# A ceiling on the density planner's rate, and a rebuilt tail, in an attention-then-density kernel

## The chip, the cores and the metric

The kernel runs on one core of a Trainium2 chip. A core has five engines that work side by side, each through its own queue in order: TensorE (PE, matrix products), VectorE (DVE, elementwise work and reductions), ScalarE (ACT, functions such as exp and tanh), GpSimd (POOL) and SyncE (SP, which here issues the DMAs). They wait for each other by semaphores. The metric is the time of one execution on the device, in microseconds (us).

## The reference, cut to what matters

The input is x, 8 images of 192 channels by 64 x 64 pixels, fp32. Two layers follow each other, each with a group norm of 32 groups of 6 channels in front and a residual around it.

```python
# layer 0: attention over the 4096 pixels of an image, on the group-normed x
q, k, v = prelu(conv1x1(gn(x), w1, b1)), prelu(conv1x1(gn(x), w2, b2)), prelu(conv1x1(gn(x), wa, ba))
x = x + softmax(q^T k) v                      # q, k: 24 channels; v: 192
# layer 1: a small network per channel, evaluated at gn(x) - 0.5 and gn(x) + 0.5
def logits(y):                                # widths 1, 3, 3, 3, 1
    for i in range(4):
        y = softplus(m[i]) @ y + b[i]
        if i < 3:
            y = y + tanh(f[i]) * tanh(y)
    return y
lower, upper = logits(gn(x) - 0.5), logits(gn(x) + 0.5)
sign = -sign(lower + upper)
x = x + max(abs(sigmoid(sign * upper) - sigmoid(sign * lower)), 1e-6)
```

The norm in front of layer 1 needs the whole attention output of an image. So the density work (layer 1) of an image can only start when its attention has ended.

## The kernel before

**The stream.** After a short head the kernel runs 1024 steps (t = 0 to 1023; `last` is 1024): 8 images (`IMG` = 128 steps), each in 8 blocks of 512 queries with 16 steps (`STEPS`), a step being one part of the keys. Image numbers start at 0 here. In a step PE computes a score tile for the next step (L780, tile sc), a score tile 22 steps ahead for the row maximum (L708, tile mx) and the product of the exponentials with the values (L795, tile b). ACT takes the exponential (L784, e from sc). DVE reduces mx to a row maximum (L716). The mx tile has one buffer, so the next L708 waits for L716.

**The planner.** All other work is laid between the steps in Python, while the program is built. `at(t, fn, ...)` puts a function under step t in `due`. `work_off(t, rate)` runs what is due, starts a job in a free PSUM tile if it can, and then calls `density_step`. There each of DVE, ACT and PE has a credit that grows by a rate in each step; due work is charged to it, and so is each density operation. Because each engine's queue is in order, the order in which the planner emits instructions is the order in which they run.

**Density work.** `Unit(b, c, g, s)` is one half-image column c, one of three channel groups g, and one sign s (lower or upper): 12 units per image, worked off in the order of a deque, up to three at a time. A unit's operations go over tiles of 128 x 1024. In the usual form it takes 16 ACT operations (first-layer tanh L1005, linear part L1014, tanh L1020, scaled copies L1030) and 23 DVE operations (all at L1037: nine mixes, then gates and adds). In the form with `on_pe` the second layer's linear part and the nine mixes are three sums on PE (`product`, L978), each of four matrix products (x and three tanhs) with diagonal weights, in one of four two-bank PSUM tiles (`banks`); then come a tanh from PSUM (L986), a gate that reads PSUM and frees it (L996), and 11 more DVE operations. Before the change, all units of the last image but the first have this form. The diagonals are built on ACT (L876: nine per group from constants; L882: three per group from the last norm).

In the stream, the density work of image b is spread over image b+1: the rate is what is left divided by the steps until 15 steps into image b+2. Buffers for tiles are 17 (`bufs`); a unit may take one only if more are free than what older units still need (`need`).

**Endings.** When both units of a column and group are done, `ending` forms the likelihood. In the stream the sum, difference and product are on POOL; near the end `alone` does them on DVE (L1187, L1196, L1197), with tanh (L1192) and Abs (L1205) on ACT, and the last add into x (L1209), after which SP stores two halves of the partitions by DMA (L1213).

**The last norm.** After the last step, `finish` scales the attention output (L815, L819), transposes it on PE (L828), adds it into x (L837) and takes statistics (L442); `norm_end` then goes in steps: aggregate (L451), mean over the group on PE (L456), differences (L462 to L466), variance on PE (L471), its sum (L477, L478), a square root on ACT (L484), and the reciprocal with one correction step (L490 to L494), and at last the weights wn (L503) and bn (L506) of the density layers. Each step stands at least one planner step after the one before; a planner step after `last` works with `RATE` = 4.15 us of DVE credit.

Of the kernel before, what the change touches and what calls it, by code (L numbers as in the profile page):

```python
# [10 lines left out]
AF = mybir.ActivationFunctionType  # L11
ALU = mybir.AluOpType
# [5 lines left out]
def kernel(  # L18
# [43 lines left out]
    nc = tc.nc  # L62

    B, C, H, W = x.shape
    N = H * W
# [812 lines left out]
    def linear_diagonals(b):  # L878
        wn, bn = norms[b, 1]
        for g in range(3):  # L880
            for i in range(3):
                nc.scalar.activation(  # L882
                    diag[g][:, 9 + i, :], ident, AF.Copy, scale=wn[:, g, 1, i : i + 1]
                )

        for s in range(2):
            d, q = lower2[:, s], lower2[:, 2 + s]
            nc.vector.tensor_copy(d, cb[:, :, 6:9])
            for j in range(3):
                nc.vector.tensor_tensor(  # L890
                    q, wsp[:, :, 12 + j : 21 : 3],
                    bn[:, s, :, 1, j : j + 1].to_broadcast([128, 3, 3]), ALU.mult,
                )
                nc.vector.tensor_tensor(d, d, q, ALU.add)
        for t in (
            *turns, ps_sc.tile([128, 2, F], F32, tag="sc", name="sc_tail"),
            ps_mx.tile([128, 2, F], F32, tag="mx", name="mx_tail"),
        ):
            banks.append(t)
    zs = {}  # L900

    class Unit:
# [3 lines left out]
        def __init__(self, b, c, g, s):  # L906
            self.key = b, c, g, s
            self.at = {}
            self.buf = {}
            self.todo = {"DVE": deque(), "ACT": deque(), "PE": deque()}  # L910
            self.left = {"l": 6, "t": 9, "u": 0, "z": 1}
            self.held = {"l": 0, "t": 0, "u": 0, "z": 0}
            self.on_pe = b == B - 1 and c + g + s > 0
            add = self.add
            if self.on_pe:

                self.left.update(t=3, u=3)
                for i in range(3):
                    add("ACT", ("u", 0, i), [], self.tanh0, makes="u")
                for i in range(3):  # L920
                    add(
                        "PE", ("sum", i), [("u", 0, j) for j in range(3)], self.product,
                        frees=[("u", 0, j) for j in range(3)] if i == 2 else [],
                    )
                    add("ACT", ("l", 1, i), [("sum", i)], self.tanh1, makes="l")
                for i in range(3):
                    add("DVE", ("gate", 1, i), [("l", 1, i)], self.gate1)
            else:
                for i in range(3):
                    add("ACT", ("t", 0, i), [], self.tanh0, makes="t")  # L930
                    add("ACT", ("l", 1, i), [], self.linear, makes="l")
                for i in range(3):
                    for j in range(3):
                        add(
                            "DVE", ("mix", i, j), [("t", 0, j), ("l", 1, i)], self.mix,
                            frees=[("t", 0, j)] if i == 2 else [],
                        )
                    add("ACT", ("t", 1, i), [("mix", i, 2)], self.tanh, makes="t")
                for i in range(3):
                    add("DVE", ("gate", 1, i), [("t", 1, i)], self.gate, frees=[("t", 1, i)])  # L940
            for i in range(3):
# [193 lines left out]
    def ending(b, c, g):  # L1135
# [6 lines left out]
        def later(n, fn, *cost):  # L1142
            at(now[0] + n, fn, *cost)
# [38 lines left out]
        def alone():  # L1182

            s = cell["s"]

            def first():
                nc.vector.tensor_tensor(s, z[0], z[1], ALU.add)  # L1187
                later(1, second, 0.0, 2.1)

            def second():  # L1190
                for i in range(2):
                    nc.scalar.activation(z[i], z[i], AF.Tanh, scale=0.5)  # L1192
                later(1, third, 2.5)

            def third():
                nc.vector.tensor_tensor(z[0], z[1], z[0], ALU.subtract)  # L1196
                nc.vector.scalar_tensor_tensor(z[0], s, 0.0, z[0], ALU.not_equal, ALU.mult)  # L1197
                bufs.extend((s, z[1]))
                later(1, size, 0.0, 1.1)
                later(2, store, 1.3)  # L1200

            later(1, first, 1.25)

        def size():
            nc.scalar.activation(z[0], z[0], AF.Abs, scale=0.5)  # L1205

        def store():
            x_ = xc[b, c][:, g, :]
            nc.vector.scalar_tensor_tensor(x_, z[0], 1e-6, x_, ALU.max, ALU.add)  # L1209
            bufs.append(z[0])  # L1210
            for i in range(2):
                k = i * N // 2 + c * 2 * F
                nc.sync.dma_start(  # L1213
                    out=ov[b, :, g, k : k + 2 * F], in_=x_[R * i : R * i + R]
                )
            if g == 2:
                xc.pop((b, c))
                free["xc"] += 1
# [155 lines left out]
    for g in range(3):  # L1374
# [5 lines left out]

# [36 lines left out]
```

## Time and profile before

| what | us |
|---|---|
| median of three runs | 4846.51 |
| lowest and highest | 4843.33, 4850.05 |
| the profiled execution | 4845.56 |
| its span, first to last instruction | 4843.8 |
| PE busy | 4656.6 (96%) |
| DVE busy | 4260.6 (88%) |
| ACT busy | 3116.6 (64%) |
| POOL busy | 523.3 (11%) |

The profile is one execution, recorded instruction by instruction. The span is cut into 40 equal slices of about 121 us; in the rows of slices a digit is the busy share of an engine in tenths, and PEclk is the clock that PE was granted. A fp32 matrix product shows as two records. The chain of waits follows the work that ended last back from the end. In timelines a line has the start, the duration, the engine, the source line, the operation and tiles, and in brackets the idle time before it with the releaser.

The largest groups of the profile:

| line, engine | count | busy us | mean ns |
|---|---|---|---|
| L795 PE | 16384 | 2966.5 | 335 |
| L780 PE | 4096 | 1155.8 | 640 |
| L708 PE | 4008 | 1132.7 | 641 |
| L716 DVE | 1002 | 1222.4 | 1220 |
| L1037 DVE, three forms | 2076 | 2652.0 | 1277 to 1300 |
| L784 ACT | 1024 | 1044.9 | 1020 |

Back to back, operations overlap a little: four of L1037 took 4.88 us on the chain of waits, 1.22 each.

### The profile page before, as it was taken

What the parts mean: (1) busy time and instruction counts of PE and PEld (TensorE: products, weight loads), DVE (VectorE), ACT (ScalarE), POOL (GpSimd) and SP (SyncE); (2) the same over time, 40 slices, a digit from 0 to 9 for tenths busy, and PEclk for the clock granted to TensorE, in tenths of its full rate; (3) what the DMA queues carried; (4) which work ended last, traced back from release to release, by engine and by line L of the source; (5) the groups of instructions that cost most, each with busy time, mean ns of one, the idle gap of its engine ahead of it and who ended that gap; (6) DMA issues with size and microseconds to landing.
All of it is one profiled execution on the core that took longest, in us unless ns stands there. A gap on an engine that the chain in (4) does not pass through costs nothing.

```text
span 4843.8 us, 68352 instructions
## 1 busy us (share of the span) xinstructions
PE 4656.6 (96%) x28384; PEld 3443.8 (71%) x28384; DVE 4260.6 (88%) x4378; ACT 3116.6 (64%) x3581; POOL 523.3 (11%) x506
## 2 busy tenths in 40 slices
PE   7999999999999999999999999999999999999496
PEld 5777777777777777777777777777777777777132
DVE  5433369999999999999999999999999999998887
ACT  2332247676767667777667766776777767777665
POOL 0000001111112111111111101111111111211000
PEclk9999999999999999999999999999999999999698
DMA  2101010001100111111110111110111100000000
GB/s 61 38 23 24 18 48 25 25 24 40 42 20 24 40 35 34 31 32 29 38 29 26 37 39 29 31 37 15 35 42 28 27 24 22 10 23 5 9 13 13
DMA packets 109163, 138.55 MB, mean 29 GB/s; under 512 B 17074, under 2 KB 82100, under 8 KB 108852
## 3 DMA queue, kind: packets, MB, share of 16 engines
q1 hardware_dynamic: 107616, 133.81, 11.0%
q8 instruction: 222, 3.64, 0.3%
q14 instruction: 89, 0.73, 0.1%
q10 hardware_dynamic: 1236, 0.37, 0.0%
HBM read 100.58 MB, written 29.36 MB: 27 GB/s over the span
## 4 chain that ended last, share of the span: by engine, by line
PE 79%; DVE 14%; ACT 4%; issue 1%; POOL 1%; DMA 0%; ACTq 0%; DVEq 0%; POOLq 0%
PE b L795 48%; PE sc L780 18%; DVE d L1037 9%; PE b L669 4%; DVE rm L716 3%; PE b L978 2%; PE b L620 1%; PE sc_tail L978 1%; PE mx_tail L978 1%; PE b L828 1%; ACT e L784 1%; PE mx L708 1%; ACT d L1005 1%; ACT d L1030 1%; ACT d L1020 1%
## 5 line engine op out<-in xcount | busy, mean ns | idle before, releaser
L795 PEld LDWEIGHTS b<-v,e 128*128 128x128 f32 x16384 | 2662.2, 191 | 779.1 <-issue 775.3
L795 PE MATMUL b<-v,e 128*128 128x193 f32 x16384 | 2966.5, 335 | 0.0
L784 ACT ACTIVATE e<-sc 128x1024 f32<-128x1024 f32 x1024 | 1044.9, 1020 | 1444.1 <-PE mx L708 1409.3
L716 DVE TENSOR_REDUCE rm<-mx 128x1 f32<-128x1024 f32 x1002 | 1222.4, 1220 | 445.9 <-PE mx L708 440.8
L780 PE MATMUL sc<-q,k 25*128 25x512 f32 x4096 | 1155.8, 640 | 22.4 <-ACT e L784 22.3
L708 PE MATMUL mx<-k,q 24*128 24x512 f32 x4008 | 1132.7, 641 | 14.1 <-DVE rm L716 13.8
L1037 DVE SCALAR_TENSOR_TENSOR d<-d,wsp,d 128x1024 f32<-128x1024 f32 x768 | 984.6, 1283 | 45.7 <-ACT d L1030 34.4
L1037 DVE SCALAR_TENSOR_TENSOR d<-d,lc,d 128x1024 f32<-128x1024 f32 x765 | 986.5, 1300 | 16.5 <-ACT d L1014 5.1
L1037 DVE SCALAR_TENSOR_TENSOR d<-d,tf,d 128x1024 f32<-128x1024 f32 x543 | 680.9, 1277 | 2.5 <-ACT d L1020 2.5
L1020 ACT ACTIVATE d<-d 128x1024 f32<-128x1024 f32 x543 | 568.0, 1053 | 65.3 <-DVE d L1037 64.7
L780 PEld LDWEIGHTS sc<-q,k 25*128 25x128 f32 x4096 | 306.4, 183 | 249.9 <-issue 189.1
L1125 POOL MEMSET pause<- 128x1 f32 x240 | 23.5, 98 | 3888.0 <-DVE d L1037 3888.0
L1030 ACT ACTIVATE d<-d,cb,wsp 128x1024 f32<-128x1024 f32 x351 | 433.4, 1235 | 2.3 <-DVE d L1037 1.7
L1005 ACT ACTIVATE d<-xc,bn,wn 128x1024 f32<-128x1024 f32 x288 | 353.6, 1234 | 12.2 <-DVE bn L506 11.4
L708 PEld LDWEIGHTS mx<-k,q 24*128 24x128 f32 x4008 | 299.9, 183 | 30.3 <-DVE rm L716 29.1
L1014 ACT ACTIVATE d<-xc,bn,wn 128x1024 f32<-128x1024 f32 x255 | 314.7, 1234 | 0.0
L1160 POOL TENSOR_TENSOR d<-d,d 128x512 f32<-128x512 f32 x80 | 173.1, 2164 | 0.7 <-issue 0.2
L1172 POOL TENSOR_TENSOR d<-d,d 128x512 f32<-128x512 f32 x80 | 167.3, 2092 | 0.4 <-issue 0.4
L1180 POOL TENSOR_TENSOR d<-d,d 128x512 f32<-128x512 f32 x80 | 161.7, 2021 | 1.9 <-ACT d L1030 0.3
L669 PE MATMUL b<-wv,xi 64*128 64x192 f32 x1344 | 139.5, 340 | 0.2 <-ACT pra L596 0.2
L669 PEld LDWEIGHTS b<-wv,xi 64*128 64x128 f32 x1344 | 106.5, 186 | 25.7 <-issue 20.2
L978 PE MATMUL b<-d,v 128*128 128x512 f32 x204 | 95.9, 622 | 17.1 <-ACT d L1005 17.1
(154 smaller groups left out, 2064.4 us busy)
## 6 DMA issues: line engine op xcount, KB each, us to landing
xi<-in_x_dram SPq DMA_DIRECT2D x280, 192.0 KB, 3.4
xc<-in_x_dram SPq DMA_DIRECT2D x64, 384.0 KB, 7.0
out_dram<-xc SPq DMA_DIRECT2D x96, 256.0 KB, 3.1
q<-qd SPq DMA_DIRECT2D x128, 128.0 KB, 2.6
k<-kq SPq DMA_DIRECT2D x64, 64.0 KB, 1.9
qd<-kq SPq DMA_DIRECT2D x64, 64.0 KB, 2.1
d<-in_x_dram SPq DMA_DIRECT2D x16, 192.0 KB, 4.6
d<-in_wat_dram ACTq DMA_DIRECT2D x2, 144.0 KB
```

Of the source, the lines that this page charges most:

```text
L669: nc.tensor.matmul(pv[:, s, 0:C], lhsT=t[p, g, k * 128 : k * 128 + 128] if g < 3 else one_row[p], rhs=wf["v", b][p, g, :] if g < 3 else wf ...
L708: nc.tensor.matmul(sc[:, s, :], lhsT=tile_of(qt[b, n // 2], n, j)[r], rhs=kt[b][r, u : u + F], start=True, stop=True,)
L716: nc.vector.tensor_reduce(out=rowmax[b, n][:, j, k : k + 1], in_=sc, axis=AX.XY, op=ALU.max)
L780: nc.tensor.matmul(sc[:, s, :], lhsT=kt[b][r, k : k + 128], rhs=qt[b, n // 2][r, :, u : u + 256], start=True, stop=True,)
L784: return lambda: nc.scalar.activation(e, sc, AF.Exp)
L795: nc.tensor.matmul(a[:, j, 0 : C + 1], lhsT=e[:, s, j * 128 : j * 128 + 128], rhs=v[:, s, p % 4, :], start=p == 0 and s == 0 and j % 2 == ...
L978: nc.tensor.matmul(out[:, h, :], lhsT=diag[g][:, 3 * i + n - 1 if n else 9 + i, :], rhs=src[:, h * F : h * F + F], start=n == 0, stop=n == 3,)
L1005: nc.scalar.activation(self.buf[k], self.src(), AF.Tanh, bias=bn[:, s, g, 0, i : i + 1], scale=wn[:, g, 0, i : i + 1],)
L1014: nc.scalar.activation(self.buf[k], self.src(), AF.Identity, bias=bn[:, s, g, 1, i : i + 1], scale=wn[:, g, 1, i : i + 1],)
L1020: nc.scalar.activation(self.buf[k], self.buf["l", k[1], k[2]], AF.Tanh)
L1030: nc.scalar.activation(self.buf[k], self.buf["l", n - 1, 0], AF.Identity, bias=offset, scale=wsp[:, g, w : w + 1],)
L1037: nc.vector.scalar_tensor_tensor(dst, src, factor, dst, ALU.mult, ALU.add)
```

## The change

It has three parts.

1. In the stream, the rate of `density_step` is at most `MOST` = 3.3.
2. `need` counts a unit's last-layer buffer (kind z) only once the unit has made its last layer-2 add.
3. The tail is rebuilt. All 12 units of the last image take the PE form. The nine constant diagonals per group are made one per step inside the last image's stream (the third group's end two steps before `last`), no longer after it; those from the norm are made for group 0 first, the others three and six steps later, and the small offsets of `lower2` move into `tail`, one step later. After `last`, planner steps have 1.3 instead of 4.15 until the last norm is ready. Up to four units are in flight instead of three, always oldest first. The very last ending works in two halves of 512 columns, with four smaller stores instead of two.

```diff
+    MOST = 3.3
...
-    def diagonals(g):
-
-        d = vtiles.pop(0).rearrange("p a b c -> p (a b c)")[:, 0 : 12 * 128]
-        d = d.rearrange("p (k n) -> p k n", k=12)
-        diag.append(d)
+    def diagonals(g, t):
+
+        def one(k):
+            if k == 0:
+                d = vtiles.pop(0).rearrange("p a b c -> p (a b c)")[:, 0 : 12 * 128]
+                diag.append(d.rearrange("p (k n) -> p k n", k=12))
+            nc.scalar.activation(diag[g][:, k, :], ident, AF.Copy, scale=lc[:, g, k : k + 1])
+
         for k in range(9):
-            nc.scalar.activation(d[:, k, :], ident, AF.Copy, scale=lc[:, g, k : k + 1])
+            at(t + k, lambda k=k: one(k), 0.0, 0.4)
...
-            self.on_pe = b == B - 1 and c + g + s > 0
+            self.on_pe = b == B - 1
...
             most = dict(self.left, t=max(0, min(self.left["t"], 1 - self.held["t"])))
+            if ("add", 2, 2, 2) not in self.at:
+
+                most.update(z=0, p=0)
             return sum(most.values())
...
             rate = left * COST["DVE"] / max(1, (units[0].key[0] + 2) * IMG + 15 - t) + OTHER
+            rate = min(rate, MOST)
...
-            order = list(range(min(3, len(units))))
-            if len(units) == 2:
+            order = list(range(min(3 if t < last else 4, len(units))))
+            if len(units) == 2 and t < last:
...
         if b == B - 1:
-            linear_diagonals(b)
+            linear_diagonals(b, 0)
+            for g in (1, 2):
+                at(now[0] + 3 * g, lambda g=g: linear_diagonals(b, g), 0.0, 1.2)
+            at(now[0] + 1, lambda: tail(b), 2.2)
...
             s = cell["s"]
+            parts = halves if (b, c, g) == (B - 1, 1, 2) else [slice(0, 2 * F)]
 
             def first():
-                nc.vector.tensor_tensor(s, z[0], z[1], ALU.add)
+                for n in parts:
+                    nc.vector.tensor_tensor(s[:, n], z[0][:, n], z[1][:, n], ALU.add)
...
-            for i in range(2):
-                k = i * N // 2 + c * 2 * F
-                nc.sync.dma_start(
-                    out=ov[b, :, g, k : k + 2 * F], in_=x_[R * i : R * i + R]
-                )
+                for i in range(2):
+                    k = i * N // 2 + c * 2 * F
+                    nc.sync.dma_start(
+                        out=ov[b, :, g, k + n.start : k + n.stop], in_=x_[R * i : R * i + R]
+                    )
...
+            else:
+
+                diagonals(0, t + 93)
+                diagonals(1, t + 104)
+                diagonals(2, last - 11)
...
-    for g in range(3):
-        at(t + 4 + g, lambda g=g: diagonals(g))
     while due or units or jobs or loads:
-        work_off(t, RATE)
+
+        work_off(t, RATE if (B - 1, 1) in norms else 1.3)
         t += 1
```

More of the change, by code (lines that the diff above doesn't have):

```diff
@@ L868, with linear_diagonals, tail @@
     lower2 = mm.rearrange("p g n -> p (g n)")[:, 0:36].rearrange("p (s g i) -> p s g i", s=4, g=3)
-    def diagonals(g):
-        d = vtiles.pop(0).rearrange("p a b c -> p (a b c)")[:, 0 : 12 * 128]
-        d = d.rearrange("p (k n) -> p k n", k=12)
-        diag.append(d)
+    def diagonals(g, t):
[4 more added lines that the diff above has]
+            nc.scalar.activation(diag[g][:, k, :], ident, AF.Copy, scale=lc[:, g, k : k + 1])
         for k in range(9):
-            nc.scalar.activation(d[:, k, :], ident, AF.Copy, scale=lc[:, g, k : k + 1])
-    def linear_diagonals(b):
+            at(t + k, lambda k=k: one(k), 0.0, 0.4)
+    def linear_diagonals(b, g):
         wn, bn = norms[b, 1]
-        for g in range(3):
-            for i in range(3):
-                nc.scalar.activation(
-                    diag[g][:, 9 + i, :], ident, AF.Copy, scale=wn[:, g, 1, i : i + 1]
-                )
+        for i in range(3):
+            nc.scalar.activation(
+                diag[g][:, 9 + i, :], ident, AF.Copy, scale=wn[:, g, 1, i : i + 1]
+            )
+    def tail(b):
+        wn, bn = norms[b, 1]
         for s in range(2):
@@ L1184, in alone @@
             s = cell["s"]
+            parts = halves if (b, c, g) == (B - 1, 1, 2) else [slice(0, 2 * F)]
             def first():
-                nc.vector.tensor_tensor(s, z[0], z[1], ALU.add)
+                for n in parts:
+                    nc.vector.tensor_tensor(s[:, n], z[0][:, n], z[1][:, n], ALU.add)
                 later(1, second, 0.0, 2.1)
             def second():
-                for i in range(2):
-                    nc.scalar.activation(z[i], z[i], AF.Tanh, scale=0.5)
+                for n in parts:
+                    for i in range(2):
+                        nc.scalar.activation(z[i][:, n], z[i][:, n], AF.Tanh, scale=0.5)
@@ L1193, in second @@
                 later(1, third, 2.5)
             def third():
-                nc.vector.tensor_tensor(z[0], z[1], z[0], ALU.subtract)
-                nc.vector.scalar_tensor_tensor(z[0], s, 0.0, z[0], ALU.not_equal, ALU.mult)
+                for n in parts:
+                    y = z[0][:, n]
+                    nc.vector.tensor_tensor(y, z[1][:, n], y, ALU.subtract)
+                    nc.vector.scalar_tensor_tensor(y, s[:, n], 0.0, y, ALU.not_equal, ALU.mult)
                 bufs.extend((s, z[1]))
-                later(1, size, 0.0, 1.1)
@@ L1200, in third, with size @@
-                later(2, store, 1.3)
+                later(1, lambda: size(parts), 0.0, 1.1)
+                later(2, lambda: store(parts), 1.3)
             later(1, first, 1.25)
[L1204 to L1209, printed above, removed]
-            bufs.append(z[0])
-            for i in range(2):
-                k = i * N // 2 + c * 2 * F
-                nc.sync.dma_start(
-                    out=ov[b, :, g, k : k + 2 * F], in_=x_[R * i : R * i + R]
-                )
+        def size(parts=(slice(0, 2 * F),)):
+            for n in parts:
+                nc.scalar.activation(z[0][:, n], z[0][:, n], AF.Abs, scale=0.5)
@@ L1216, in store @@
+        def store(parts=(slice(0, 2 * F),)):
+            for n in parts:
+                x_ = xc[b, c][:, g, n]
+                nc.vector.scalar_tensor_tensor(x_, z[0][:, n], 1e-6, x_, ALU.max, ALU.add)
+                for i in range(2):
+                    k = i * N // 2 + c * 2 * F
+                    nc.sync.dma_start(
+                        out=ov[b, :, g, k + n.start : k + n.stop], in_=x_[R * i : R * i + R]
+                    )
+            bufs.append(z[0])
             if g == 2:
@@ L1373 @@
     homes[:] = [(turns[1], [0, 0])]
-    for g in range(3):
-        at(t + 4 + g, lambda g=g: diagonals(g))
     while due or units or jobs or loads:
-        work_off(t, RATE)
+        work_off(t, RATE if (B - 1, 1) in norms else 1.3)
         t += 1
```

## The prediction

> **What bounds the kernel now.** I read the slices of the page first, then the windows of the last 364 us, then the order of time on each engine at two places: an image boundary and the tail.
>
> ```profile
> PE   7999999999999999999999999999999999999496
> DVE  5433369999999999999999999999999999998887
> PEclk9999999999999999999999999999999999999698
> ```
>
> From slice 7 to 37 both PE and DVE show nines, so either could be the bound. The starts of the exp activations tell them apart: most of the 1024 steps are 3.88 us apart, which is PE's pace (L795 2.81 on the chain, L780 and L708 side by side, 1.06). DVE idles about 16 us per image there. But at a boundary of two images the chain leaves PE and runs over DVE (1778 to 1813 us). The timelines of DVE and of PE (start, us, engine and line, count, and in brackets the wait before):
>
> ```profile
> 1805.04 0.55 DVE L442 BATCH_NORM_STATS2 st<-xi 128x6 f32<-128x384 f32 x1
> 1805.50 3.66 DVE L1037 SCALAR_TENSOR_TENSOR d<-d,tf,d 128x1024 f32<-128x1024 f32 x3
> 1809.08 2.67 DVE L1037 SCALAR_TENSOR_TENSOR d<-d,lc,d 128x1024 f32<-128x1024 f32 x2
> 1811.66 1.22 DVE L716 TENSOR_REDUCE rm<-mx 128x1 f32<-128x1024 f32 x1
> ```
>
> ```profile
> 1812.94 1.69 PE L708 MATMUL mx<-k,q 24*128 24x512 f32 x4 [2.77 <-DVE rm L716]
> 1814.56 5.52 PE L795 MATMUL b<-v,e 128*128 128x193 f32 x16
> ```
>
> Five density operations stand between two reduces, so L708 waits 2.77 us for a free bank; the next L795 then takes 5.52 instead of 2.88. By the exp starts the six steps 12 to 17 of image 3 take 34.7 us; at PE's pace they would take 23.3. The same shape stands at the starts of images 2 to 6, five times. At image 7, where the burst is weaker, they take 28.3.
>
> The end, in four stages (columns: span, then busy us and count of PE, PEld, DVE, ACT, POOL, clock, DMA):
>
> ```profile
> 4480.00:4531.20 51.20, 2.71 (x10) 2.14 (x10) 49.32 (x57) 32.75 (x55) 0.00 (x0) 0.53 0.04 10
> 4531.20:4564.40 33.20, 24.80 (x49) 10.43 (x50) 27.96 (x38) 25.61 (x30) 0.00 (x0) 0.76 0.06 17
> 4564.40:4807.20 242.80, 213.71 (x481) 92.06 (x479) 199.90 (x163) 158.41 (x147) 0.00 (x0) 0.96 0.03 9
> 4807.20:4843.80 36.60, 0.07 (x1) 0.00 (x0) 26.02 (x22) 14.05 (x13) 0.00 (x0) 0.54 0.11 29
> ```
>
> For 51 us after the last attend (4479.6, call it E) PE stands still and DVE is full: the steps of the last norm lie in one DVE queue with image 6's density.
>
> ```profile
> 4479.61 0.18 DVE L815 RECIPROCAL rc<-b 128x4 f32<-128x4 f32 x1
> ...
> 4520.02 0.15 DVE L477 TENSOR_TENSOR ve<-nrm,b 128x1 f32<-128x1 f32 x1
> ...
> 4530.89 0.23 DVE L503 TENSOR_SCALAR wn<-wx,nrm 128x18 f32<-128x18 f32 x1
> ```
>
> Then PE is the bound. A unit has three sums of 6.87 us, but the chain shows a period of 22.65 (starts at 4652.26, 4674.94, 4697.55, 4720.22), because of one wait per unit:
>
> ```profile
> 4648.84 1.11 ACT d L986
> 4649.95 1.12 ACT d L1030
> 4651.07 1.14 ACT d L1005
> 4652.22 0.04 issue
> 4652.26 12.28 PE b L978 x28
> ```
>
> The tanh of the finished sum, a scaled copy and only then the next unit's first tanh stand in ACT's queue: PE has the four xc records (1.7 us) to cover 3.4.
>
> **What the Trainium skill says.** "TensorE: Matmul & The Clock Gate", Part 1, has PE's clock halved after an idle window of about 3.4 us until one busy window has passed. The trace agrees in kind: 5.52 against 2.88 after the boundary, though there the idle time was only 2.77. "Perfetto Trace Analysis", Optimization Strategy, says that a regime has its own most-contended engine; the slices at boundary and tail show it. "ScalarE: Activation LUTs", What ACT_TABLE_LOAD costs, gives 1283 ns; the trace has 1.28. I use the trace's.
>
> **Part 1, the ceiling of 3.3.** Nothing is added or removed; DVE operations move. I counted, in the order of instructions of both programs, what stands between successive reduces at the start of image 3, steps 9 to 17: before 2,3,2,1,3,5,2,2,2; after 2,2,2,1,2,2,2,3,2. Four fewer at 1.21 us: 4.8 us leave the stretch where DVE is the path (images 4 to 6 lose the same four, image 2 four in steps 4 to 17). They come later at about one per 30 steps, where DVE has its 16 us of idle time per image; I charge 0.7 for steps they delay. The half clock after the stall cost 2.6 (L795) and some 0.5 (L708 1.69 for 1.13); a shorter stall keeps part of it away, I take 1.5. So 4.8 + 1.5 - 0.7 = 5.6 per boundary, times five: 28. Nearly the same comes from image 7's 28.3 for 34.7 (6.4). Lower bound 0 (DVE is 97% busy, a deferral may only shift the wait); upper 8 each, 40. Images 1 and 7 hardly change.
>
> **Part 2, buffers counted later** (z only after its last layer-2 add). It lets a younger unit take a buffer sooner; no instruction changes. Cost 0, with 5 to either side for reordered ACT work.
>
> **Part 3, the tail.** Steps of 1.3 put one density operation between norm steps instead of three. From L815 to wn the order has 34 L1037 operations before, 8 after: 26 x 1.22 = 31.7 less. Walking the rest (evacuation behind two L1192, transposes 1.54, residual 0.87, statistics 1.0 and 0.8, small steps, table load 1.28, sqrt 0.2) with the trace's durations gives wn at E+21 instead of E+51.4. The 26 operations now stand after the norm, partly ahead of the first gates.
>
> The first nine-copy diagonals, 27 copies in 7.98 us, move into image 7's stream, one of 0.3 per step behind an exp. ACT waits for PE there, so 0; uncovered it is 8. Of the nine last copies only three now precede the first sum.
>
> First unit: its tanhs follow ten ACT operations, several waiting for adds. I get the third tanh at E+39, the first sum at E+41, two more of 6.87, and 2 for the half clock: third sum at E+57. Before it was 4564.4, E+84.8. The second unit's tanhs stand amid image 6's rest: 24 us; the third, with an Abs ahead, 23.5. From the fourth on, ACT again has tanh of the sum, scaled copy, three tanhs, so I take 22.65 for nine units, 203.9. Last sum: 57 + 24 + 23.5 + 203.9 = E+308.4. Before: E+327.6 with one unit fewer on PE; that unit costs a full period, and the former 23 DVE operations become 14, which is 11 us off a DVE that isn't the bound.
>
> Can DVE follow? A unit is 14 operations and two of endings, 16 x 1.22 = 19.6 in 22.65: yes. Banks: four, freed by gates that follow the tanh by about 2.5 us: no wait.
>
> After the last sum: tanh 1.1, gate 1.3, then six adds, three gates and two adds with ACT's tanhs between, to +20.5; the ending in halves takes 5.6 instead of 8.15 (1.24 + 2.01 + 2.5 + 1.06 + 1.23, with hops). Last store at 26.1 after the last sum, before 31.8. Four DMAs of half the size replace two; nothing stands behind them on SP; the last 4.8 us stay. Tail gain: 19.2 + 5.7 = 24.9; bounds 10 (each stage 5 worse) and 40 (the tanh wait of 1.8 goes away in eight units).
>
> **Sum.** 28 + 25 = 53 against the profiled execution's 4845.6 (span 4843.8 and 1.8 around it): 4792.6, called 4793. That execution is 0.9 under the median 4846.5, which I leave.
>
> **Rivals.**
> A, one part brings nothing: either DVE's total is the limit in the stream (97% busy speaks for it; 3.88 us steps, PE's own pace, against), or image 6's rest delays the first unit as much as the norm gained. 4845.6 - 26 = 4819.
> B, the tail is better: with four units in flight the tanhs come early and PE runs at 20.6 per unit; 9 x 2 less, 4775. ACT's order speaks against it.
> C, slower: four units in one in-order ACT and DVE queue make a convoy; tanh waits for adds, adds for gates, gates for sums. The profile has one: from 4564.4 to 4600.4 a unit took 36 us, 13.4 over the period, while units of both kinds mixed. From a mean excess of 53/11 = 4.8 us per unit (period 27.5) it decides; five units at 36 us give 4793 + 67 = 4860. Against it: the counted order has at most one such mix, at the start.
> D, no net effect: 4846, for instance both gains eaten by reordering.
>
> **How the numbers follow.** Forecast 0.60, A 0.25, B 0.07, C 0.06, D 0.02. A range from 4773 (B) to 4823 (A with its own spread) leaves C, D and the outer parts of A and B out, under 0.2. What this kernel's measurement can tell from no change is about 0.2%, 10 us: faster 0.92, within 0.02, slower 0.06.
>
> **What would show it.** Right: no L708 wait over 1.5 us at 1810, 2370 and so on; images 2 to 6 some 5.6 us shorter by the exp starts; wn about 21 us after the last attend; sums of three every 22.65; last sum near 308. Wrong: DVE waits of PE spread over the stream, half clock still at each boundary, a third sum later than E+65, or ACT waits for DVE inside a unit in steady state.

## The result, and the profile after

The changed kernel takes 4802.47 us (median of three runs, 4801.80 to 4803.81) against 4846.51: a ratio of 0.9909, 95% interval 0.9887 to 0.9932. That is 44 us less; the forecast was 53 less.

The profiled execution's span fell from 4843.8 to 4800.7 us. I cut both spans at the first exp (L784) and at E, the end of the last attend, which is 4479.6 in the trace before and 4458.1 in the trace after:

| part of the span | before, us | after, us | difference |
|---|---|---|---|
| head, to the first exp | 91.2 | 95.7 | +4.6 |
| stream, first exp to E | 4388.4 | 4362.3 | -26.1 |
| tail, E to the end | 364.2 | 342.6 | -21.6 |

The change puts nothing into the head and takes nothing out of it; its 4.6 us are taken up under the hardware at the end, and so is the chance in the stream's 26.1. Stream and tail together give 47.7 less. The slices of the page after:

```profile
PE   7999999999999999999999999999999999999696
...
DVE  5433359999999999999999999999999999999888
...
PEclk9999999999999999999999999999999999999898
```

The single weak slice of PE near the end now has a 6 where it had a 4, with the clock at 8 instead of 6: the pause around the last norm is shorter.

**The boundary of two images.** DVE after the change, at the place where five L1037 stood between two reduces (the density lines are six higher in the changed kernel, L1037 is L1043 and the first tanh L1005 is L1011; in the kernels with the ceiling alone they are one higher):

```profile
1801.16 1.23 DVE L716 TENSOR_REDUCE rm<-mx 128x1 f32<-128x1024 f32 x1
1802.31 0.55 DVE L442 BATCH_NORM_STATS2 st<-xi 128x6 f32<-128x384 f32 x1
1802.77 2.59 DVE L1043 SCALAR_TENSOR_TENSOR d<-d,wsp,d 128x1024 f32<-128x1024 f32 x2
1805.28 1.22 DVE L716 TENSOR_REDUCE rm<-mx 128x1 f32<-128x1024 f32 x1
```

Two density operations stand there now, and the reduces come 4.1 us apart. The view of waits, over 150 to 4440 us (engine, line waited for, then us in total, times, longest), has before

```profile
PE sc L780 <- ACT e L784: 20.0, 26, 2.1
...
PE mx L708 <- DVE rm L716: 13.8, 5, 2.8
```

and after

```profile
PE sc L780 <- ACT e L784: 31.5, 29, 2.3
```

The wait of L708 for DVE is gone from the list, all five of it. But the wait of L780 for the exp grew by 11.5 us. PE and ACT show the largest of those at the same boundary:

```profile
1794.76 2.88 PE L795 MATMUL b<-v,e 128*128 128x193 f32 x16
1799.93 0.70 PE L780 MATMUL sc<-q,k 25*128 25x512 f32 x2 [2.29 <-ACT e L784]
...
1801.00 2.88 PE L795 MATMUL b<-v,e 128*128 128x193 f32 x16
```

```profile
1792.55 1.06 ACT L1026 ACTIVATE d<-d 128x1024 f32<-128x1024 f32 x1 [0.37 <-DVE d L1043]
1795.47 1.24 ACT L1011 ACTIVATE d<-xc,bn,wn 128x1024 f32<-128x1024 f32 x1 [1.86 <-DVE bn L506]
1796.61 1.23 ACT L1020 ACTIVATE d<-xc,bn,wn 128x1024 f32<-128x1024 f32 x1
1797.74 1.23 ACT L1011 ACTIVATE d<-xc,bn,wn 128x1024 f32<-128x1024 f32 x1
1798.88 1.00 ACT L784 ACTIVATE e<-sc 128x1024 f32<-128x1024 f32 x1
```

The first tanh of the next image's density (L1011) stands ahead of an exp in ACT's queue, waits 1.86 us for the norm's bn, and brings two more operations along (a linear part, L1020, and a second tanh) before the exp may run. PE waits for that exp.

**The tail,** in the four windows that answer to those before (E to the new weights, to the first unit's third sum, to the last sum, to the end; the same columns):

```profile
4458.00:4480.10 22.10, 2.78 (x11) 2.15 (x10) 19.13 (x33) 10.99 (x14) 0.00 (x0) 0.58 0.09 24
4480.10:4516.20 36.10, 24.69 (x49) 10.48 (x50) 31.65 (x41) 21.30 (x26) 0.00 (x0) 0.74 0.00 1
4516.20:4767.80 251.60, 229.84 (x529) 99.01 (x527) 220.55 (x181) 175.35 (x163) 0.00 (x0) 1.00 0.04 11
4767.80:4800.70 32.90, 0.00 (x0) 0.00 (x0) 22.86 (x23) 12.36 (x14) 0.00 (x0) 0.56 0.13 32
```

The first stage fell from 51.2 to 22.1 us. The third holds 529 PE records instead of 481, the sums of the unit that DVE did before, in 8.8 us more. The chain of waits still has one pause per unit:

```profile
4586.74 1.11 ACT d L992
4587.85 1.13 ACT d L1036
4588.98 1.14 ACT d L1011
4590.12 0.04 issue
4590.16 12.28 PE b L984 x28
```

After the last sum PE has nothing left to do, and DVE (22.9 us busy) and ACT (12.4) share the stage. It begins on DVE like this:

```profile
4767.96 2.60 DVE L1043 SCALAR_TENSOR_TENSOR d<-d,wsp,d 128x1024 f32<-128x1024 f32 x2
4770.48 1.27 DVE L1002 SCALAR_TENSOR_TENSOR d<-d,tf,mx_tail 128x1024 f32<-128x1024 f32 x1
4771.67 2.60 DVE L1043 SCALAR_TENSOR_TENSOR d<-d,wsp,d 128x1024 f32<-128x1024 f32 x2
4776.52 2.60 DVE L1043 SCALAR_TENSOR_TENSOR d<-d,wsp,d 128x1024 f32<-128x1024 f32 x2 [2.25 <-ACT d L1036]
```

The gate (L1002) of the last sum waits behind two older adds, and starts 2.7 us after that sum ended at 4767.8. From that end to the end of the span it is 32.9 us, before 36.5.

### The profile page after: what moved, and what is told of

Read it like the earlier page. It is cut to its first block, busy times and chain, and to the rows that moved or that the text cites. A ratio compares the mean times of both kernels' runs of the same rounds, so it can differ in the third digit from the quotient of the medians.

```text
span 4800.7 us, 68448 instructions
## 1 busy us (share of the span) xinstructions
PE 4653.7 (97%) x28432; PEld 3444.5 (72%) x28432; DVE 4244.4 (88%) x4373; ACT 3112.0 (65%) x3581; POOL 530.4 (11%) x506
## 4 chain that ended last, share of the span: by engine, by line
PE 82%; DVE 11%; ACT 5%; issue 1%; DMA 0%; POOL 0%; SPq 0%; ACTq 0%; DVEq 0%; POOLq 0%
PE b L795 51%; PE sc L780 19%; DVE d L1043 7%; PE b L669 4%; DVE rm L716 3%; PE b L984 2%; PE b L620 2%; PE mx_tail L984 1%; ACT d L1011 1%; PE sc_tail L984 1%; ACT e L784 1%; ACT d L1020 1%; ACT d L1036 1%; PE mx L708 1%; PE b L828 1%
## 5 line engine op out<-in xcount | busy, mean ns | idle before, releaser
L795 PEld LDWEIGHTS b<-v,e 128*128 128x128 f32 x16384 | 2655.5, 190 | 776.7 <-issue 770.6
L795 PE MATMUL b<-v,e 128*128 128x193 f32 x16384 | 2959.4, 334 | 0.0
L784 ACT ACTIVATE e<-sc 128x1024 f32<-128x1024 f32 x1024 | 1045.6, 1021 | 1421.1 <-PE mx L708 1381.6
L780 PE MATMUL sc<-q,k 25*128 25x512 f32 x4096 | 1154.9, 640 | 33.9 <-ACT e L784 33.7
L708 PE MATMUL mx<-k,q 24*128 24x512 f32 x4008 | 1130.0, 640 | 0.0
L1043 DVE SCALAR_TENSOR_TENSOR d<-d,wsp,d 128x1024 f32<-128x1024 f32 x768 | 985.3, 1284 | 52.5 <-ACT d L1036 41.8
L1043 DVE SCALAR_TENSOR_TENSOR d<-d,lc,d 128x1024 f32<-128x1024 f32 x756 | 972.2, 1294 | 16.1 <-ACT d L1020 2.4
L1043 DVE SCALAR_TENSOR_TENSOR d<-d,tf,d 128x1024 f32<-128x1024 f32 x540 | 681.2, 1286 | 3.7 <-ACT d L1026 3.7
L780 PEld LDWEIGHTS sc<-q,k 25*128 25x128 f32 x4096 | 306.2, 183 | 261.3 <-issue 181.6
L1138 POOL MEMSET pause<- 128x1 f32 x240 | 23.5, 98 | 3855.4 <-DVE d L1043 3855.4
L1011 ACT ACTIVATE d<-xc,bn,wn 128x1024 f32<-128x1024 f32 x288 | 353.4, 1234 | 12.3 <-DVE bn L506 11.5
L1020 ACT ACTIVATE d<-xc,bn,wn 128x1024 f32<-128x1024 f32 x252 | 311.3, 1235 | 0.0
L708 PEld LDWEIGHTS mx<-k,q 24*128 24x128 f32 x4008 | 299.8, 183 | 4.8 <-DVE rm L716 4.7
L669 PEld LDWEIGHTS b<-wv,xi 64*128 64x128 f32 x1344 | 106.5, 186 | 25.4 <-issue 19.0
```

The costliest lines, as they stand in the source:

```text
L669: nc.tensor.matmul(pv[:, s, 0:C], lhsT=t[p, g, k * 128 : k * 128 + 128] if g < 3 else one_row[p], rhs=wf["v", b][p, g, :] if g < 3 else wf ...
L708: nc.tensor.matmul(sc[:, s, :], lhsT=tile_of(qt[b, n // 2], n, j)[r], rhs=kt[b][r, u : u + F], start=True, stop=True,)
L780: nc.tensor.matmul(sc[:, s, :], lhsT=kt[b][r, k : k + 128], rhs=qt[b, n // 2][r, :, u : u + 256], start=True, stop=True,)
L784: return lambda: nc.scalar.activation(e, sc, AF.Exp)
L795: nc.tensor.matmul(a[:, j, 0 : C + 1], lhsT=e[:, s, j * 128 : j * 128 + 128], rhs=v[:, s, p % 4, :], start=p == 0 and s == 0 and j % 2 == ...
L1011: nc.scalar.activation(self.buf[k], self.src(), AF.Tanh, bias=bn[:, s, g, 0, i : i + 1], scale=wn[:, g, 0, i : i + 1],)
```

## The experiments

All times are medians; ratios are against the kernel before, run beside them (4847.46 to 4848.36 in these sessions).

### Each part alone

The ceiling alone, on the kernel before:

```diff
+    MOST = 3.3
             rate = left * COST["DVE"] / max(1, ...) + OTHER
+            rate = min(rate, MOST)
```

> The kernel before with the ceiling of 3.3 alone. Theory (the ceiling takes the density burst off the six boundary steps, so DVE no longer holds PE there): images 2 to 6 each some 5 us shorter by the exp starts, no wait of L708 for DVE over 1 us, about 4821. Rival 1 (the later count of buffers does it, the ceiling only moves work): images as before, 4846. The last 364 us unchanged in either.

Measured: 4815.78 us (4812.85 to 4820.53), ratio 0.9935 (0.9918 to 0.9951). The stream is 33.2 us shorter, the tail 1.3, and no wait of L708 is left in the list. It is more than my 28, and more than the stream gains in the full change.

The later count alone:

```diff
         most = dict(self.left, ...)
+        if ("add", 2, 2, 2) not in self.at:
+            most.update(z=0, p=0)
```

> The kernel before with only the later count of the last-layer buffer. Theory (it costs about nothing, or a few us because ACT work is bunched and exp comes late): the five waits of L708 for DVE of 2.8 us stay, 4841 to 4856. Rival 1 (this is what shortens the stream): 4821.

Measured: 4833.24 us (4830.93 to 4835.98), ratio 0.997 (0.9959 to 0.9982). The theory, that it is worth nothing, falls. The five waits of L708 stay, as it said (14.2 us in all). The stream gave 3.8 us and the tail 10.2. PE's timeline shows the place in the tail, first before:

```profile
4568.04 1.98 PE L978 MATMUL mx_tail<-d,v 128*128 128x512 f32 x4 [1.80 <-ACT d L1005]
4581.08 5.63 PE L978 MATMUL mx_tail<-d,v 128*128 128x512 f32 x8 [11.06 <-ACT d L1005]
```

then with the later count:

```profile
4565.82 5.42 PE L978 MATMUL mx_tail<-d,v 128*128 128x512 f32 x12 [1.81 <-ACT d L1005]
```

Before, the second unit got one first-layer tanh, and PE waited 11 us for the other two, which ACT began at 4579.80. With z counted later ACT does the three in one go, and the second unit takes 22.7 us instead of 35.9. The edit changes nothing but the count of buffers, so it was this count that had held them back. My prediction had seen this 36 us unit (rival C quotes it) and didn't ask which of the three parts would remove it.

The rebuilt tail alone:

```diff
 (the kernel after)
-            rate = min(rate, MOST)
-        if ("add", 2, 2, 2) not in self.at:
-            most.update(z=0, p=0)
```

> The rebuilt tail alone, without ceiling and later count. Theory (the two gains are independent): stream as before with its five waits, wn about 22 us after the last attend, last sum about 310, in all 22 less: 4824. Rival (the tail needs the later count of buffers, since four units share 17 buffers): the period of three sums is over 22.65, last sum at 320 or later, 4834 or more.

Measured: 4830.71 us (4826.16 to 4832.16), ratio 0.9963 (0.9948 to 0.9978), between both expectations. The tail is 17.8 us shorter. The stream is 4.4 longer, but that is chance: it lies in images 1 and 2, while the edit first touches image 7, which takes 516.6 us in both. So the 27 copies of the diagonals cost the stream nothing, as predicted. The second unit takes 33.4 us here, the old stall again.

The full change without the later count:

```diff
 (the kernel after)
-        if ("add", 2, 2, 2) not in self.at:
-            most.update(z=0, p=0)
```

> The changed kernel without the later count of buffers. Theory (that count bunches ACT work, which shows as L780 waiting for exp, 31.5 us in the changed kernel against 20.0 before): those waits fall by 5 to 12 us, 4790 to 4799, unless the tail loses as much. Rival (the waits come from the ceiling's own reordering): 4802 within 3.

Measured: 4798.61 us (4794.54 to 4800.32), ratio 0.99 (0.9885 to 0.9915). It is 3.9 us faster than the full change by the medians, though the two intervals of the ratio overlap. Its second unit takes 31.7 us against 24.1 after, but its first unit's third sum comes 4.2 us sooner, and its last sum stands at E+312.1 against E+309.7: beside the rebuilt tail the later count is worth 2.4 us. In the stream it costs: L780 waits 23.5 us for exps here, as with the ceiling alone, and 31.5 with the count. That it costs is seen in more than this pair: five traces with ceiling and count have streams of 4361.3 to 4367.8 us, two with the ceiling and the rebuilt tail but without the count in the stream 4360.0 and 4360.1. Alone, on the kernel before, the same count lowered these waits from 20.0 to 15.8 us, so it is beside the ceiling that it costs. I take it that a younger unit's ACT operations come ahead of an exp sooner; no run shows that apart.

Together: by their ratios the three parts alone give 31, 15 and 18 us, in sum 64; the full change gave 44. By the traces the stream gives 32.6 us in the three runs together and 26.1 in the full change, the tail 29.3 and 21.6. In the stream the later count, which gave 3.8 us alone, takes some 4 beside the ceiling, and the 4.4 of the rebuilt tail are chance. In the tail the count is worth 10.2 us alone and 2.4 behind the rebuilt tail: it takes 7.6 us off the second unit there, and the first unit's third sum comes 4.2 later. Why it comes later I did not follow.

### The pieces of the tail

The long steps again before the last norm:

```diff
-        work_off(t, RATE if (B - 1, 1) in norms else 1.3)
+        work_off(t, RATE)
```

> The changed kernel with steps of 4.15 instead of 1.3 before the last norm. Theory (PE's start after the norm sets the end): wn back to E+45 to 51, the third sum 15 to 28 us later, 4817 to 4828. Rival (DVE's total after the last attend sets the end, the order does not matter): 4802 within 4.

Measured: 4816.05 us (4815.03 to 4819.14), ratio 0.9935 (0.992 to 0.995). The weights wn come at E+49.5 instead of E+21.9, 27.6 us later, but the end comes only 12.7 later, and the time is one microsecond short of the expected 4817. Image 6's rest, done ahead of the norm, no longer lies between the first units: the third sum is 16.4 us later, and the second unit takes 20.6 us, PE's own three sums, instead of 24.1. So the tail gains about 9 us without the short steps. What the other pieces are worth (the order of the diagonals, the last ending in halves) was not run apart.

The last image's first unit back on DVE:

```diff
-            self.on_pe = b == B - 1
+            self.on_pe = b == B - 1 and c + g + s > 0
```

> The changed kernel with the last image's first unit in the old form (nine mixes on DVE, no sums on PE), so 33 sums. Theory (a unit on PE costs a full period, but a unit with nine mixes at the start delays the first gates, as in the kernel before): within 10 of the changed kernel, 4795 to 4812; if the mixes hide, a period of 22.65 is saved and it is nearer 4785. Rival (all units on PE is what shortened the tail): 4815 or more.

Measured: 4808.69 us (4803.44 to 4810.10), ratio 0.992 (0.9906 to 0.9935). Its last sum comes 6.1 us later, though PE has three sums fewer.

Three units in flight instead of four:

```diff
-            order = list(range(min(3 if t < last else 4, len(units))))
+            order = list(range(min(3, len(units))))
```

> The changed kernel with three units in flight instead of four. Theory (the period of 22.65 comes from ACT's order tanh of the sum, scaled copy, next tanhs, which three units have too): steady period the same, only the start differs, 4800 to 4810. Rival (the fourth unit is what keeps PE fed at the start): third to sixth sum 10 us or more longer, 4812 or more.

Measured: 4800.54 us (4795.78 to 4805.31), ratio 0.9908 (0.9891 to 0.9924). The sums end at the same places and the tail is again 342.6 us. The fourth unit is worth nothing here.

### The level of the ceiling

If only the step with five DVE operations costs, a ceiling that merely removes that step must do as well:

```diff
+    MOST = 4.5
+            rate = min(rate, MOST)
```

> The kernel before with a ceiling of 4.5 instead of 3.3, alone. It leaves three operations at most in a boundary step, where 3.3 leaves two and no ceiling five. Theory (only the step of five operations makes PE wait, and the half clock follows it): most of the gain stays, L708 waits under 1 us, steps 12 to 17 at 26 to 30, 4816 to 4826. Rival (the level of 3.3 matters, since the run-up to the boundary is DVE-bound too): half the gain or less, 4830 or more.

Measured: 4841.77 us (4835.82 to 4847.79), ratio 0.9988 (0.9982 to 0.9995): 6 us instead of some 30, and the rival's "4830 or more" came. The theory falls, although the trace shows what was meant. L708 waits only 0.9 us in all, and steps 12 to 17 of images 2 to 6 take 28.7 us in the mean instead of 33.6. By the starts of the exps (us, mean of images 2 to 6, one execution each; that of 4.5 was the slowest of its twenty, 6 us over their median):

| steps | before | 4.5 alone | 3.3 alone |
|---|---|---|---|
| 12 to 15 | 18.8 | 18.8 | 19.1 |
| 16 and 17 | 14.8 | 9.9 | 7.9 |
| 24 to 27 | 16.9 | 19.4 | 15.3 |
| whole image | 556.1 | 555.7 | 550.0 |

Of the 5.7 us per image that 4.5 lacks against 3.3, 1.7 lie in steps 12 to 17 and 4.1 in steps 24 to 27. First the boundary. Steps 16 and 17 still have three density operations ahead of the reduce, so L708 starts 1.0 and 1.3 us after the L780 beside which it should run, and the pair takes up to 2.4 us instead of 1.06:

```profile
1808.34 1.13 PE L780 MATMUL sc<-q,k 25*128 25x512 f32 x4
1809.39 1.13 PE L708 MATMUL mx<-k,q 24*128 24x512 f32 x4
...
1813.26 1.13 PE L780 MATMUL sc<-q,k 25*128 25x512 f32 x4
1814.56 1.13 PE L708 MATMUL mx<-k,q 24*128 24x512 f32 x4 [0.18 <-DVE rm L716]
```

No wait of L708 is listed for the first of these, since PE is still busy with L780. At 4.5 four L708 of a boundary start 0.8 to 1.3 us late, at 3.3 one does. Then the rest of the image. What step 17 gained is given back: 2.5 us in steps 24 to 27, 1.0 of it half clock (a stretch for which the profile records half of PE's clock) that follows in three of the five images, and some 1 us each in steps 48 to 55 and 72 to 79 (with 3.3 the second of these is there too). Step 24 takes 7.9 us, where before it took 6.3 in four of the five images, with this on ACT (the kernel with 4.5, ACT's timeline):

```profile
1843.73 1.02 ACT L784 ACTIVATE e<-sc 128x1024 f32<-128x1024 f32 x1 [1.80 <-PE sc L780]
1844.78 1.28 ACT L484 ACT_TABLE_LOAD   x1
1846.07 0.20 ACT L484 ACTIVATE sq<-ve 128x1 f32<-128x1 f32 x1
1847.22 1.06 ACT L1207 ACTIVATE d<-d 128x1024 f32<-128x1024 f32 x1 [0.94 <-POOL d L1182]
1848.29 1.28 ACT L1021 ACT_TABLE_LOAD   x1
1849.58 1.06 ACT L1021 ACTIVATE d<-d 128x1024 f32<-128x1024 f32 x1
1850.55 1.23 ACT L1031 ACTIVATE d<-d,cb,wsp 128x1024 f32<-128x1024 f32 x1
1851.68 1.00 ACT L784 ACTIVATE e<-sc 128x1024 f32<-128x1024 f32 x1
```

A square root between two tables, an Abs that waits for POOL, and two density operations all stand between two exps. To test that this is where the time went, the planner books more of ACT for the square root of the attention's norm, which moves the tanh and the scaled copy behind the exp and nothing at the boundary:

```diff
 (the kernel with MOST = 4.5)
-            at(now[0] + 1, root, 0.0, 2.8)
+            at(now[0] + 1, root, 0.0, 2.8 if key[1] or not stream[0] else 6.0)
```

> The kernel with the ceiling at 4.5, where in addition the planner books 6.0 us instead of 2.8 on ScalarE for the step with the square root of the attention's norm (step 24 of an image). In the order of instructions this moves two density operations (a tanh and a scaled copy, 2.3 us) out of the stretch before the exp of step 25 and nothing in the boundary steps 12 to 17. Theory: what the ceiling of 4.5 gains at the boundary (step 17 of 11 us gone) is partly lost in step 24, which grew to 7.9 us in its trace because ScalarE has table load, square root, a wait for POOL of 0.9, Abs, table load, tanh and scaled copy between two exps. Then step 24 falls to about 5.6, some 2 us in each of five images, and the time lies at 4826 to 4835 (the kernel with 4.5 alone had 4841.8). Rival: the two operations only crowd the next steps (25 to 27, with the three scaled weights), and the time stays at 4838 to 4846; then the pace of VectorE in the three boundary steps with a late maximum matmul is all that keeps 4.5 from 3.3.

Measured: 4832.23 us (4827.53 to 4833.20), ratio 0.9965 (0.9951 to 0.9978): 9.5 us better, as the theory said. In its trace the same exp comes 6.0 us after the one before:

```profile
1839.53 1.02 ACT L784 ACTIVATE e<-sc 128x1024 f32<-128x1024 f32 x1 [1.80 <-PE sc L780]
...
1843.01 1.06 ACT L1207 ACTIVATE d<-d 128x1024 f32<-128x1024 f32 x1 [0.94 <-POOL d L1182]
1844.23 1.28 ACT L784 ACT_TABLE_LOAD   x1 [0.16 <-PE mx L708]
1845.52 1.02 ACT L784 ACTIVATE e<-sc 128x1024 f32<-128x1024 f32 x1
```

Steps 24 to 27 take 16.8 us, about what they took before, and images 2 to 6 are 2.7 us shorter each than with 4.5 alone, while steps 12 to 17 are the same. "ScalarE: Activation LUTs", What ACT_TABLE_LOAD costs, has 1283 ns for a load and a drain of about 1380 ns beside it. The load is 1.28 here; no drain of that size shows, since the square root starts 0.01 us after its load.

So a ceiling pays by more than the removal of one step: at 3.3 three of the four late L708 are gone as well, and ACT's crowded step takes 4.5 us instead of 7.9.

### Versions that beat both kernels

The next version goes at the pause that is left in each unit of the steady chain. It lets the next unit's first tanhs come right behind the oldest unit's ACT work, without regard to ACT's credit, and gives them three more buffers from tiles that are free in the tail:

```diff
-            while todo and credit[eng] > 0:
+            while todo and (credit[eng] > 0 or todo[0][0][0] == "u"):
...
+            if eng == "ACT" and t >= last:
+                order.sort(key=lambda n: 0.5 if n and units[n].todo[eng] and units[n].todo[eng][0][0][0] == "u" else n)
...
+    for v in vtiles:
+        bufs.append(v.rearrange("p a b c -> p (a b c)")[:, 0 : 2 * F])
```

> The changed kernel with, in the tail, a unit's three first tanhs put before the tanh of the last sum of the unit ahead, as soon as buffers allow, and three more buffers made from value tiles that the attention no longer needs. Theory (the wait of 1.8 to 2.0 us per unit for the next unit's first tanh is all that parts PE from its own pace of 20.6): period down to about 20.8 where the tanhs are early, last sum 10 to 18 us sooner, 4786 to 4793. Rival (DVE, 19.6 us per unit, then becomes the limit, or the tanhs ahead delay ACT's other work): no gain, 4800 to 4810.

Measured: 4780.81 us (4776.23 to 4785.55), ratio 0.9865 (0.985 to 0.988), better than expected. Its chain runs over PE alone across unit after unit:

```profile
4559.91 6.87 PE b L984 x16
4566.78 6.87 PE sc_tail L984 x16
4573.65 6.87 PE mx_tail L984 x16
4580.51 13.73 PE b L984 x32
```

In these lines a unit takes 20.6 us, three sums of 6.87. The tail is 321.7 us, 21 less than after, but not by the period alone: the first unit's third sum comes 12.6 us sooner, at E+45.6, the second unit takes 20.6 us and the third 31.8 (8 more), the other nine 185.7 instead of 203.8, and from the last sum to the end it is 38.0 instead of 32.9. Order and buffers weren't run apart, so which of the two weighs more is open.

The same, with the later count only in the tail, since the stream lost by it:

```diff
-        if ("add", 2, 2, 2) not in self.at:
+        if now[0] >= last and ("add", 2, 2, 2) not in self.at:
```

> The tail with early tanhs and three more buffers, the ceiling, and the later count of buffers only after the last step, so that the stream is that of the run without the later count. Theory (the later count costs the stream 2 to 7 us by late exps and gains only in the tail): 4774 to 4779. Rival (the difference of those streams is chance of half-clock stretches): 4781 within 3.

Measured: 4774.69 us (4769.98 to 4777.55), ratio 0.9851 (0.9836 to 0.9865), 6.1 us better. The trace puts 5.4 in the stream, of which 1.7 is less half clock, which is chance; so the theory and the rival each have a part.

And ACT booked for the step of the density norm, so that fewer first operations stand ahead of the exp at the boundary:

```diff
-            at(now[0] + 2, fourth, 1.5)
+            at(now[0] + 2, fourth, 1.5, 3.5 if key[1] and stream[0] else 0.0)
```

> The same as the run before it, and in the stream the planner step that finishes a density norm is charged 3.5 us on ACT, so that fewer density operations stand between the square root and the next exp. Theory (what is left at a boundary is L780 waiting 1.2 to 2.3 us for an exp that is queued behind table loads and behind first tanhs that wait for bn, and the half clock that can follow): steps 12 to 17 fall from about 26.5 to 28 towards 24 to 25, six times, 4762 to 4771. Rival (the table loads alone make the wait): within 3 of the run before it.

Measured: 4771.65 us (4766.67 to 4774.23), ratio 0.9844 (0.9829 to 0.9859), the fastest by its median, but just outside the theory's 4762 to 4771 and 3.0 us from the run before it, which is the rival's bound. The two runs overlap, so the time alone doesn't decide; the traces show what was meant. ACT at the boundary:

```profile
1786.94 1.02 ACT L784 ACTIVATE e<-sc 128x1024 f32<-128x1024 f32 x1 [0.52 <-PE sc L780]
1789.62 1.24 ACT L1036 ACTIVATE d<-d,cb,wsp 128x1024 f32<-128x1024 f32 x1 [1.67 <-DVE d L1043]
1790.77 1.23 ACT L1011 ACTIVATE d<-xc,bn,wn 128x1024 f32<-128x1024 f32 x1
1791.90 1.00 ACT L784 ACTIVATE e<-sc 128x1024 f32<-128x1024 f32 x1
```

The wait for bn is no longer ahead of an exp. L780's waits for exps fell to 12.0 us in all, the longest 1.0, and steps 12 to 17 of images 2 to 6 take 25.4 us in the mean, in the run before it 27.0.

## Why the prediction was right, and where its sizes were off

**The mechanism of Part 1 was right.** The five-operation step went, and the five waits of L708 went. The half clock went only in part. At images 3 and 4 L795 takes 2.88 us after the boundary; at images 2, 5 and 6 a wait of L780 for an exp takes the place of L708's, and a half-clock record of 3.4 us follows it, so one of my signs of being wrong came at three boundaries of five. At image 5:

```profile
2899.90 0.70 PE L780 MATMUL sc<-q,k 25*128 25x512 f32 x2 [2.29 <-ACT e L784]
...
2900.97 4.56 PE L795 MATMUL b<-v,e 128*128 128x193 f32 x16
```

The records at the five boundaries fell from 23.9 to 10.2 us. At half speed that is worth some 6.9 us (an estimate from these two figures), 1.4 per boundary where I took 1.5. In the full change, steps 12 to 17 of images 2 to 6 lost 29.4 us in sum (my 4.8 + 1.5, five times, is 31.5), and these images as a whole 24.4. So 1.0 us per image came back elsewhere where I had charged 0.7. With the ceiling alone the same sums are 33.3 and 30.6: 6.1 per image against my 5.6. My sum was thus near, but for the ceiling alone; in the full change Part 2 took some of it, and chance moves both by a few us.

**Part 2 at nothing was right as a sum and wrong in its ground.** I took 0 with 5 to either side. In the full change that holds: 2.4 us gained in the tail, some 4 lost in the stream, 3.9 slower by the medians. But "no instruction changes" was no ground for it. Alone it is worth 15 us, most of it the second unit's stall in the old tail, and the 24 us that I gave the second unit under Part 3 rest on it: without it that unit takes 31.7. That it came out near 0 is luck: a gain in the tail and a loss in the stream nearly cancel, and of the two I had thought only of the reordered ACT work. The time it moves lies in who may take a buffer, and that never shows in a count of operations.

**Part 3's walk held within about 1 us in every stage but the last.** Relative to E, predicted and measured:

| point | predicted | after |
|---|---|---|
| wn | 21 | 21.9 |
| first unit's third sum | 57 | 58.2 |
| second unit | 24 | 24.1 |
| third unit | 23.5 | 23.6 |
| nine units | 203.9 | 203.8 |
| last sum | 308.4 | 309.7 |
| last sum to the end | 30.9 | 32.9 |

The mis-sized term is the last. I let the gate follow 1.1 us after the last sum, by the tanh alone; it started at 2.7, behind two older adds. In the profile before it had already stood at 2.5 (L996 at 4809.77, the sum's end at 4807.27), so I could have seen it. The adds then ended at +22.4 instead of +20.5, the ending took 6.0 instead of 5.6, and the last DMA 4.5 instead of 4.8. Tail gain: 21.6 instead of 24.9. The price of the short steps was in the walk, and the run with long steps shows it: of the 27.6 us that they gain at wn, 11 are lost again before the third sum and 3.5 in the second unit, where image 6's rest now lies.

**What is left of the gap** between 53 and the span's 43 less: 2 in the stream, 3 in the tail, and 4.6 in the head, which has no part in the change. By the medians the gap is 9. The 2 in the stream are less than the chance in it.

**The rivals.** A, that one part brings nothing, is out: the ceiling and the rebuilt tail each gain alone. B's state, PE at 20.6 per unit, doesn't come with four units in flight, as the prediction said from ACT's order; it comes when that order and the buffers are changed. C's convoy didn't appear: no unit takes over 24.1 us, and what the profile of before had as its germ was a lack of buffers. D is out.

## What to carry to other kernels

In this kernel the cap on a burst was worth what it cleared on every engine, not in one step. So look for the steps in which other queues already have a table load or a foreign wait, and for pairs of matrix products that run one after the other without a listed wait. When a planner may hand out a scarce buffer sooner, price it by who waits for buffers in the trace, in each stage apart: the same rule gained in the tail and, beside the ceiling, lost in the stream. What parts gain alone need not add up (64 us here, and 44 together), so before summing them ask what each leaves for the others to gain.

## What the runs showed of the hardware

The head's length varied from one execution to the next, though no edit touches it: over the fourteen profiled executions the first exp came 91.1 to 91.8 us after the start in five, 93.3 to 93.8 in four, and 95.1 to 97.4 in five. Between 60 and 100 us the mean granted clock was 0.96 in the five shortest heads and 0.91 in the five longest, but 1.00 in one of the middle ones, so the clock there is not all of it.

The stream varied too. Five of the kernels here (the full change, and those with long steps, the first unit on DVE, three units, early tanhs) have the same order of operations on ACT, DVE and POOL up to E, yet their streams took 4361.3 to 4367.8 us. The half-clock records in these streams sum up to 17.1 to 30.7 us. Half of that taken off, as an estimate of what half speed costs, leaves 4351.8 to 4352.8: nearly all of the difference is half clock. The same sum for the three with the ceiling and without the later count in the stream (the ceiling alone, the full change without the count, and the one with the count only in the tail) gives 4348.0 to 4348.4, so the count costs the stream some 4 us. For the kernel before it gives 4367.9: about 10 of the 26 us that the stream gained are less half clock. So up to 6 us in the head and as much in the stream, between two single profiles of this kernel, mean nothing, and stages have to be compared one by one.

"TensorE: Matmul & The Clock Gate", Part 1, ties the half clock to an idle window of about 3.4 us that runs freely. In the stream after the change the half-clock records are 3.4 us long, which agrees. But none of the 29 waits of PE listed there is longer than 2.3 us, and there are six such records all the same; of the boundary waits of 2.29 us, those at 2899.9 and 3453.0 are followed by a record within 2 us, those at 1799.9 and 2349.9 by none. So in these traces a listed wait shorter than that window may cost the clock or not, with nothing in the program to tell which. The two matrix products beside such a wait use few rows of the array (24 and 25); whether that counts as idle no run shows.
